# Half of the second batch's query and key projection moved into its first attention group, and two routings one group later

## The chip, the cores and the metric

The kernel runs on one core of a Trainium2 chip. A core has TensorE (PE, with its weight loads shown apart as PEld), VectorE (DVE), ScalarE (ACT), GpSimd (POOL) and SyncE (SP), each with a queue that it works through in order, and sixteen DMA engines. The metric is the device time of one launch in microseconds (us).

## The reference

The kernel computes one transformer layer on two batches of 2048 tokens with 256 channels. Cut to what matters:

```
qkv = (x @ Wqkv + bqkv).reshape(B, L, 3, 16, 16)
scores = einsum('bqhd,bkhd->bhqk', q, k) / 4 - slope[h] * |pos_q - pos_k|
x = layernorm(x + softmax(scores) @ v @ Wout + bout)
weights = softmax(x @ router_w.T + router_b)            # 8 experts, the last a no-op
per token the two best experts; each of 7 experts takes its first 512 tokens
x = layernorm(x + sum over its experts of weight * relu(x @ W1[e]) @ W2[e] + no-op part)
```

## The kernel before

**Attention.** The work is cut into units (b, g): batch b, group g of four heads; g counts from 0, so the change's "groups 3 and 4" are g = 2 and 3. A unit has four blocks n of 512 queries. (The last three units are split: blocks 0 to 2 of (1,1), (1,2), (1,3) come first, then their blocks 3.) A block is a row of steps. A step makes scores for two pairs of heads on PE (L699), their exponential on ACT (L707, mostly 128 x 1024), where the keys are near the queries a multiplication by a table of distances on DVE (L712), and two steps later the product with the values on PE (L615) into a PSUM accumulator. In groups 1 to 3 only a block's own four key tiles are multiplied by the table; group 0 (steep slopes) has few key tiles, and each piece of them is multiplied. At a block's end DVE divides (done), and after the odd group of a pair project_out adds the output projection to x_all (L509, L511). Score tiles and all side work share three PSUM tiles (tag st); accumulators have two.

**Projection.** project_qk(b, m, i, xb) makes queries and keys of a chunk i of 512 tokens for half m of the heads: m = 0 serves groups 0 and 1, m = 1 groups 2 and 3. For keys and then queries (a = 1, 0): two matmuls (L289), the high half hi with bias (L294 on ACT or L296 on DVE), the low half lo on DVE (L297), and their writes to DRAM (kd, qd) from SP (L300). Then POOL squares hi (L304), PE sums the squares (nrm, L310), and DVE takes the maximum (n, L317). project_v makes the values. project_all(b) (L349) goes over the four chunks and does m = 0, m = 1 and v of each; for batch 1 it is called second. find_flag (L361) reduces all these maxima, with two PE transposes in a chain with DVE, to a flag for a general path that is not taken here.

**Routing.** route(b, n) does for a block of 512 tokens: layer norm on DVE, transposes (rt, L745), logits (lg, L754), exponential (L784) and choice of the experts on DVE (some 25 small operations), counts (cnt, L826), slots on DVE, and eight scatters from POOL (L855). It starts when project_out of the second pair of groups has added its part.

**Order.** PE and ACT run in the order in which the program is written (manual_schedule, L880). DVE, POOL and SP are ordered by a scheduler at build time. Side work is written as generators: later(gen) puts one on a list, and pump (L488), called once at the end of each step, advances the first that is due; a generator that yields k is due k steps later, one that yields None lets the next one go. finish(gen) runs a generator to its end on the spot. second is put on the list after unit (0,1) and finished before the last block of (0,3), where the keys of (1,0) are loaded; find_flag is put on it after (0,3). After (1,0) the pools of the projection (x, hi, lo, sq) are closed, and the memory goes to the experts' weights (load_expert).

**Experts.** After attention seven experts run one after the other (L1195 to L1219), with gathers and scatters from POOL.

Of the kernel before, what the change touches and what calls it, by code (L numbers as in the profile page):

```python
# [22 lines left out]
G = 4  # L23
# [4 lines left out]
NQB = L // QB  # L28
# [94 lines left out]
def fast_path(  # L123
# [25 lines left out]
    def st_tile(name):  # L149
        return ps_st.tile([P, 2, QB], F32, tag="st", name=name)  # L150
# [23 lines left out]
    def load_x(b, i):  # L174
        xb = p_x.tile([P, 2, QB], F32, tag="xb", name=f"xb_{b}_{i}")
        nc.sync.dma_start(out=xb, in_=xt[b].rearrange("(c p) l -> p c l", p=P)[:, :, i * QB : (i + 1) * QB])
        return xb
# [103 lines left out]
    def project_qk(b, m, i, xb, queue=nc.sync):  # L281

        n0 = f"{b}_{m}_{i}"
        hi = p_s.tile([P, 2, QB], F32R, tag="hi", name=f"hi_{n0}")
        lo = p_s.tile([P, 2, QB], F32R, tag="lo", name=f"lo_{n0}")
        for a, dst in ((1, kd), (0, qd)):
            ps = st_tile(f"qk_{n0}_{a}")
            for c in range(2):
                nc.tensor.matmul(  # L289
                    ps[:, 0, :], wqk_sb[:, a, c, m * P : (m + 1) * P], xb[:, c, :], start=(c == 0), stop=(c == 1)  # L290
                )
            bias = bqk_sb[:, a, m : m + 1]
            if (b, m) == (0, 0):
                nc.scalar.activation(hi[:, a, :], ps[:, 0, :], AF.Identity, bias=bias)  # L294
            else:
                nc.vector.tensor_scalar(hi[:, a, :], ps[:, 0, :], bias, None, ALU.add)  # L296
            nc.vector.scalar_tensor_tensor(lo[:, a, :], ps[:, 0, :], bias, hi[:, a, :].bitcast(F32), ALU.add, ALU.subtract)  # L297
            for r, half in enumerate((hi, lo)):
                for to in (dst[b][m][i][:, c, :, r, :] for c in range(2)) if a else (dst[b][m][i][:, r, :, :],):
                    queue.dma_start(out=to, in_=half[:, a, :].bitcast(F32))  # L300
            yield 2
        sq = p_s1.tile([P, 2, QB], F32, tag="sq", name=f"sq_{n0}")
        hf = hi.bitcast(F32)
        nc.gpsimd.tensor_tensor(sq, hf, hf, ALU.mult)  # L304
        yield 6
        ps = st_tile(f"nrm_{n0}")

        for a in range(2):
            for c in range(4):
                nc.tensor.matmul(  # L310
                    ps[32 * c : 32 * c + 32, 0, a * P : (a + 1) * P],
                    blk,
                    sq[:, a, c * P : (c + 1) * P],
                    start=True,
                    stop=True,
                )
        nc.vector.tensor_reduce(  # L317
            n2[:, b, m, :, i], ps[:, 0, 0 : 2 * P].rearrange("p (a t) -> p a t", a=2), AX.X, ALU.max
        )
# [26 lines left out]
        if keep is not None:  # L346
            keep(vs)

    def project_all(b):  # L349
        xb = load_x(b, 0)  # L350
        for i in range(NQB):
            xb_next = load_x(b, i + 1) if i + 1 < NQB else None
            yield 1
            for m in range(2):
                yield from project_qk(b, m, i, xb)
                yield 2
            yield from project_v(b, i, xb)
            yield 2
            xb = xb_next

    def find_flag():  # L361

        mx = small.tile([P, 2, B, 2], F32, tag="mx", name="mx")
        top = small.tile([P, 1], F32, tag="mxt", name="mxt")
        for a in range(2):
            nc.vector.tensor_reduce(mx[:, a, :, :], n2[:, :, :, a, :], AX.X, ALU.max)
        nc.vector.tensor_reduce(top, vm.rearrange("p b i h -> p (b i h)"), AX.X, ALU.max)
        yield 4

        ps = st_tile("flag_s")  # L370
        for a in range(2):
            nc.tensor.transpose(ps[0:4, a, 0:P], mx[:, a, :, :].rearrange("p b m -> p (b m)"), ident)
        nc.tensor.transpose(ps[0:1, 0, P : 2 * P], top, ident)
        by_head = small.tile([4, 2, 32], F32, tag="mxh", name="mxh")
        nc.vector.tensor_reduce(by_head, ps[0:4, :, 0:P].rearrange("p a (c h) -> p a h c", c=4), AX.X, ALU.max)
        nc.vector.tensor_tensor(by_head[:, 0, :], by_head[:, 0, :], by_head[:, 1, :], ALU.mult)
        high = small.tile([4, 1], F32, tag="mx4", name="mx4")
        nc.vector.tensor_reduce(high, by_head[:, 0, :], AX.X, ALU.max)

        nc.vector.tensor_scalar(high, high, 0.99 / (4 * SMALL_SCORE) ** 2 / 0.98, None, ALU.mult)  # L380
        two = small.tile([1, 2], F32, tag="two", name="two")
        nc.vector.tensor_reduce(two[:, 0:1], ps[0:1, 0, P : 2 * P], AX.X, ALU.max)
        nc.vector.tensor_scalar(two[:, 0:1], two[:, 0:1], 1.0 / SMALL_V**2, None, ALU.mult)
        yield 4
        ps = st_tile("flag_t")
        nc.tensor.transpose(ps[0:1, 0, 0:4], high, ident[0:4, 0:4])
        nc.vector.tensor_reduce(two[:, 1:2], ps[0:1, 0, 0:4], AX.X, ALU.max)
        one = small.tile([1, 1], F32, tag="one", name="one")
        nc.vector.tensor_reduce(one, two, AX.X, ALU.max)
        nc.vector.tensor_scalar(bad[:, 0:1], one, 1.0, None, ALU.is_gt)  # L390
# [87 lines left out]
        return mixed(steps, own, 3 if n == 2 else 2)  # L478

    step = 0  # L480

    keys_in, queries_in, values_in = [0], [0], []
    waiting = []

    def later(gen, wait=0):
        waiting.append([step + wait, gen])
# [13 lines left out]
    def finish(gen):  # L500
        for w in [w for w in waiting if w[1] is gen]:
            waiting.remove(w)
        for _ in gen:
            pass
# [11 lines left out]
    def key_order(blocks):  # L516
        return (1, 2, 3, 0) if blocks[0] == 0 else (2, 1, 0, 3)
# [23 lines left out]
    def load_unit(b, g, blocks):  # L541
        ks, vu = unit_tiles(b, g, blocks)

        with tc.issue_after(last["q"].ins):
            for i in key_order(blocks):
                load_keys(b, g, i, ks)
            for i in range(NQB):
                load_values(b, g, i, vu)
        return ks, vu
# [173 lines left out]
    def route(b, n):  # L723
# [2 lines left out]

        rests = (5, 2, 2, 5) if (b, n) == (B - 1, NQB - 2) else (7, 3, 3, 9)
        while len(routed) < NQB * b + n - 1:
            yield None
        t0 = b * TB + 4 * n  # L730
        n0 = f"{b}_{n}"
# [195 lines left out]
    def first_blocks():  # L927


        one = project_qk(0, 0, 1, xbs[1])  # L930
        next(one)
        load_keys(0, 0, 1, ks)
# [61 lines left out]
        load_rest()  # L994
    make_fill()
    loaded = (ks, vu), first_tables, q_first
    second = project_all(1)
    for u, (b, g, blocks) in enumerate(units):
        (ks, vu), (e_t, f_t), q_t = loaded
        fs = None if f_t is None else (f_t[:, 0, :], f_t[:, 1, :])  # L1000
        va = va_first if u == 0 else None
        for n in blocks:
            if u in (1, 2):
                with tc.issue_after(last["q"].ins):
                    load_residual(NQB * (u - 1) + n)
            if u == 1 and n == 2:
                with tc.issue_after(last["q"].ins):
                    clear_slots()
            if g or va is None:
                va = values(b, g, n, vu)  # L1010
            if u == 0 and n + 1 in blocks:
                q_next = None
            elif n + 1 in blocks:
                q_next = load_q(b, g, n + 1)
            elif u + 1 < len(units):
                nb, ng, nblocks = units[u + 1]
                if (nb, ng) == (0, 2):
                    finish(other_half)
                if (nb, ng) == (1, 0):
                    finish(second)  # L1020
                nxt = load_unit(nb, ng, nblocks)
                q_next = load_q(nb, ng, nblocks[0])
            block(b, g, n, ks, va, e_t, fs, q_t)
            if q_next is None:
                while n + 1 not in queries_in:
                    pump()
                q_next = load_q(b, g, n + 1)
            q_t = q_next
        if u + 1 < len(units):
            loaded = nxt, load_tables(nb, ng), q_next  # L1030
        if (b, g) == (0, 1):
            later(second)
        if (b, g) == (0, G - 1):
            later(find_flag())
        if (b, g) == (1, 0):
            pctx.close()
            p_w = ctx.enter_context(tc.tile_pool(name="p_w", bufs=2, side="right"))
            expert_w = {0: load_expert(0)}
            p_x0 = ctx.enter_context(tc.tile_pool(name="p_x0", bufs=1, side="right"))
# [739 lines left out]
```

## Time and profile before

| what | us |
|---|---|
| median of three timed runs (1205.15 to 1208.55) | 1207.42 |
| the profiled execution, time | 1196.63 |
| its span, first to last instruction | 1194.8 |
| PE busy in it (93%) | 1114.9 |
| ACT busy (67%) | 796.7 |
| DVE busy (60%) | 714.6 |
| POOL busy (24%) | 284.5 |
| mean granted TensorE clock | 0.967 |

Units begin with their first exponential at 239.0 us (0,2), 382.6 (0,3), 541.4 (1,0), 620.5 (1,1), 695.8 (1,2) and 785.3 (1,3). A row of the profile's groups gives the line, engine, operation, output and inputs, shapes and count, then busy time and mean duration, then the idle time of the engine just before such instructions and what ended it. Shares of busy time over the whole span hide that the stages have different limits, so the stretches are looked at apart. A PE that is shown busy is not always at its peak, since the ends of matmuls are modelled.

### The profile page before, as it was taken

Reading aid. Unit: us, or ns where it says so; the run is one execution under the profiler, and the core shown is the slowest. Engines: PE = TensorE matmul, PEld = TensorE weight load, DVE = VectorE, ACT = ScalarE, POOL = GpSimd, SP = SyncE. Lnnn points to the kernel's source line nnn. Section 1 sums busy time; section 2 is a strip of 40 time slices with the busy share of each in tenths; the row PEclk is TensorE's granted clock in tenths of the full one; section 3 lists DMA queues with packets and bytes.
Section 4 is the critical chain, followed back from the end, with each engine's and each line's share of the span. In section 5 each row is a group of like instructions: output and inputs, shape, how many; then the busy total and the mean of one; then the engine's idle time right before and its main releaser. Section 6 shows DMA issues by size and latency. Waiting matters only on the chain. (4 is left out here: it accounts for less than half of the span.)

```text
span 1194.8 us, 19048 instructions
## 1 busy us (share of the span) xinstructions
PE 1114.9 (93%) x7174; PEld 495.6 (41%) x7174; DVE 714.6 (60%) x1525; ACT 796.7 (67%) x902; POOL 284.5 (24%) x304
## 2 busy tenths in 40 slices
PE   8788899999999999986989999999999999999996
PEld 3454334333323343433533333223334237666664
DVE  3738667754565467778985654446788543216534
ACT  4444588888887887673559999999886961112510
POOL 1111322222210112224164111111142402222253
PEclk9988899999999999997899999999999999999998
DMA  5648474342523314454334122122356413348721
GB/s 182 233 165 259 161 243 149 109 170 89 176 90 122 128 47 137 128 196 156 114 129 145 53 102 71 54 102 71 98 195 213 174 55 106 102 141 269 247 74 52
DMA packets 108147, 164.53 MB, mean 138 GB/s; under 512 B 28432, under 2 KB 59792, under 8 KB 108048
## 3 DMA queue, kind: packets, MB, share of 16 engines
q1 hardware_dynamic: 96960, 140.04, 36.0%
q0 software_dynamic: 5952, 16.49, 3.9%
q10 hardware_dynamic: 5136, 6.71, 1.7%
q8 instruction: 59, 0.97, 0.3%
q14 instruction: 40, 0.33, 0.1%
HBM read 108.86 MB, written 54.35 MB: 137 GB/s over the span
## 5 line engine op out<-in xcount | busy, mean ns | idle before, releaser
L707 ACT ACTIVATE pr<-s 128x1024 f32<-128x1024 f32 (+2 forms) x796 | 733.8, 1095 | 183.3 <-PE s L699 177.2
L712 DVE TENSOR_TENSOR pr<-pr,e 128x1024 f32<-128x1024 f32 (+16 forms) x366 | 341.8, 975 | 189.5 <-ACT pr L707 188.1
L699 PE MATMUL s<-q,k 64*128 64x512 f32 (+11 forms) x1852 | 330.2, 432 | 23.6 <-DMA k<-kd 8.3
L699 PEld LDWEIGHTS s<-q,k 64*128 64x128 f32 x1852 | 153.8, 189 | 334.3 <-ACT pr L707 229.9
L615 PE MATMUL acc_B<-pr,va 128*32 128x512 f32 (+5 forms) x1080 | 139.0, 570 | 0.0
L615 PE MATMUL acc_A<-pr,va 128*32 128x512 f32 (+8 forms) x1080 | 138.8, 569 | 0.0
L1202 ACT ACTIVATE ht<-h 128x1024 f32<-128x1024 f32 x28 | 28.7, 1023 | 143.5 <-PE h L1195 143.0
L615 PE MATMUL acc_D<-pr,va 128*32 128x512 f32 x768 | 113.5, 604 | 4.5 <-DVE wX L652 2.2
L589 POOL TENSOR_TENSOR va<-vu,fk_sb 128x768 f32<-128x768 f32 (+2 forms) x36 | 40.8, 1134 | 282.1 <-PE acc_D L615 267.3
L1216 PE MATMUL y<-w,ht 128*128 128x256 f32 x448 | 98.1, 379 | 2.2 <-DVE ye L1219 2.2
L1195 PE MATMUL h<-xet,w 128*128 128x512 f32 x224 | 97.9, 593 | 1.4 <-issue 1.4
L1216 PEld LDWEIGHTS y<-w,ht 128*128 128x128 f32 x448 | 84.6, 190 | 14.2 <-DVE ye L1219 2.6
L615 PE MATMUL acc_E<-pr,va 128*32 128x512 f32 (+15 forms) x696 | 69.5, 412 | 20.4 <-DVE pr L712 20.2
L855 POOL DMA_INDIRECT xbuf<-x_all,slot x56 | 62.2, 1110 | 97.4 <-DVE top L847 50.4
L304 POOL TENSOR_TENSOR sq<-hi 128x1024 f32<-128x1024 f32 x16 | 31.0, 1938 | 184.1 <-DVE hi L296 146.1
L289 PE MATMUL qk<-xb,wqk_sb 128*128 128x512 f32 x128 | 65.3, 633 | 1.1 <-ACT v L339 0.6
L1195 PEld LDWEIGHTS h<-xet,w 128*128 128x128 f32 x224 | 42.3, 190 | 50.8 <-issue 49.7
L1219 DVE SCALAR_TENSOR_TENSOR ye<-y,xe,sums 128x256 f32<-128x256 f32 x28 | 13.5, 484 | 64.7 <-PE y L1216 62.3
L1083 POOL DMA_INDIRECT sums<-abuf,to x28 | 26.9, 962 | 78.4 <-DVE to L1077 38.2
L615 PEld LDWEIGHTS acc_E<-pr,va 128*32 128x32 f32 x696 | 24.7, 117 | 46.6 <-DVE pr L712 22.0
L615 PEld LDWEIGHTS acc_B<-pr,va 128*32 128x32 f32 x1080 | 25.3, 108 | 42.5 <-issue 40.8
L615 PEld LDWEIGHTS acc_A<-pr,va 128*32 128x32 f32 x1080 | 24.8, 108 | 41.0 <-issue 39.2
(162 smaller groups left out, 870.5 us busy)
## 6 DMA issues: line engine op xcount, KB each, us to landing
k<-kd SPq DMA_DIRECT2D x86, 256.0 KB
e<-in_c_e SPq DMA_DIRECT2D x10, 1920.0 KB
q<-qd SPq DMA_DIRECT2D x62, 256.0 KB
w<-in_w SPq DMA_DIRECT2D x14, 1024.0 KB
kd<-hi SPq DMA_DIRECT2D x32, 256.0 KB
kd<-lo SPq DMA_DIRECT2D x32, 256.0 KB
xb<-in_xt SPq DMA_DIRECT2D x12, 512.0 KB
vu<-vd SPq DMA_DIRECT2D x40, 128.0 KB
```

Of the source, the lines that this page charges most:

```text
L289: nc.tensor.matmul(ps[:, 0, :], wqk_sb[:, a, c, m * P : (m + 1) * P], xb[:, c, :], start=(c == 0), stop=(c == 1))
L304: nc.gpsimd.tensor_tensor(sq, hf, hf, ALU.mult)
L589: nc.gpsimd.tensor_tensor(va[:, t0:t1, :, 0:HD], v4[:, t0:t1], fb, ALU.mult)
L615: nc.tensor.matmul(blk_["acc"](to)[32 * row : 32 * row + 32, q0:q1], blk_["va"][:, t, j, :], pr[:, jj, c0 : c0 + q1 - q0], start=key not i ...
L699: nc.tensor.matmul(ps[:, jj, c0 : c0 + q1 - q0], ks[hp][t // 4][r, t % 4 * P : (t % 4 + 1) * P], q_t[r, hp, q0:q1], start=True, stop=True,)
L707: nc.scalar.activation(pr[:, :, 0:w], ps[:, :, 0:w], AF.Exp, scale=1.0 / math.sqrt(HD))
L712: nc.vector.tensor_tensor(pc, pc, e_t[:, 2 * hp : 2 * hp + 2, x0 : x0 + q1 - q0], ALU.mult)
L855: nc.gpsimd.indirect_dma_start(out=xbuf_by[4 * k + u], out_offset=bass.IndirectOffsetOnAxis(ap=slot_i[:, k, u : u + 1], axis=0), in_=x_all ...
L1083: nc.gpsimd.indirect_dma_start(out=sums[:, s, :], out_offset=None, in_=abuf[:, :], in_offset=bass.IndirectOffsetOnAxis(ap=to[:, s : s + 1] ...
L1195: nc.tensor.matmul(ps[:, a, :], w1_sb[:, c, (2 * f + a) * P : (2 * f + a + 1) * P], xet[:, c, :], start=(c == 0), stop=(c == 1),)
L1202: nc.scalar.activation(ht[:, 2 * f : 2 * f + 2, :], ps, AF.Relu)
L1216: nc.tensor.matmul(ps, ht[:, f, s * P : (s + 1) * P], w2_sb[:, f, :], start=(f == 0), stop=(f == NC - 1))
```

## The change

- project_all is split. project_most(b) does for each chunk m = 0 and v. project_others(b) loads the chunks of x again and does m = 1, one step less apart, and then find_flag.
- second is now project_most(1), in its old place. third is project_others(1). It is put on the list after (0,3), where find_flag was, and finished before the last block of (1,0), where the keys of (1,1) are loaded.
- hi is made on ACT where b == m, so for (0, 0) as before and now for (1, 1); for (0, 1) and (1, 0) it is made on DVE as before.
- route(0, 2) and route(0, 3) wait until unit number 5, which is (1,1).

```diff
-            if (b, m) == (0, 0):
+            if b == m:
                 nc.scalar.activation(hi[:, a, :], ps[:, 0, :], AF.Identity, bias=bias)
...
-    def project_all(b):
+    def project_most(b):
+
         xb = load_x(b, 0)
         for i in range(NQB):
             xb_next = load_x(b, i + 1) if i + 1 < NQB else None
             yield 1
-            for m in range(2):
-                yield from project_qk(b, m, i, xb)
-                yield 2
+            yield from project_qk(b, 0, i, xb)
+            yield 2
             yield from project_v(b, i, xb)
             yield 2
             xb = xb_next
+
+    def project_others(b):
+        xb = load_x(b, 0)
+        for i in range(NQB):
+            xb_next = load_x(b, i + 1) if i + 1 < NQB else None
+            yield 1
+            yield from project_qk(b, 1, i, xb)
+            yield 1
+            xb = xb_next
+        yield from find_flag()
...
     step = 0
+    at_unit = 0
...
         while len(routed) < NQB * b + n - 1:
+            yield None
+
+        while (b, n) in ((0, 2), (0, 3)) and at_unit <= G:
             yield None
...
-    second = project_all(1)
+    second, third = project_most(1), project_others(1)
     for u, (b, g, blocks) in enumerate(units):
+        at_unit = u
...
                 if (nb, ng) == (1, 0):
                     finish(second)
+                if (nb, ng) == (1, 1):
+                    finish(third)
...
         if (b, g) == (0, G - 1):
-            later(find_flag())
+            later(third)
```

## The prediction

> **What bounds the kernel now.** I read the page's groups first, then busy time by stretch, then the timeline of the places the change touches. Counting the exponentials (L707, in program order) cuts the time into blocks (batch, group, block of queries). Rows of the stretches: start:end, length, then busy us of TensorE (PE), its weight loads, VectorE (DVE), ScalarE (ACT), GpSimd (POOL), then clock, DMA share, GB/s.
>
> ```profile
> L707 ACT ACTIVATE pr<-s 128x1024 f32<-128x1024 f32 (+2 forms) x796 | 733.8, 1095 | 183.3 <-PE s L699 177.2
> 239.02:278.19 39.17, 38.37 (x232) 12.82 (x224) 21.95 (x26) 30.10 (x33) 7.59 (x8) 1.00 0.42 143
> 278.19:311.06 32.87, 32.48 (x230) 11.57 (x232) 15.56 (x21) 29.55 (x32) 7.75 (x10) 1.00 0.30 100
> 311.06:347.60 36.54, 35.64 (x228) 10.88 (x224) 21.49 (x25) 30.05 (x34) 9.13 (x7) 1.00 0.44 135
> 347.60:382.61 35.01, 34.54 (x228) 12.11 (x228) 19.19 (x21) 29.86 (x33) 4.18 (x7) 1.00 0.35 113
> 382.61:417.71 35.10, 34.65 (x226) 10.65 (x224) 16.79 (x22) 29.83 (x33) 7.07 (x8) 1.00 0.43 149
> 417.71:455.89 38.18, 38.17 (x262) 15.93 (x260) 27.34 (x51) 30.21 (x33) 3.71 (x8) 1.00 0.14 45
> 455.89:499.90 44.01, 42.86 (x274) 16.82 (x272) 35.36 (x93) 30.40 (x33) 9.14 (x7) 0.96 0.44 137
> 499.90:541.35 41.45, 36.71 (x250) 15.59 (x252) 29.05 (x97) 29.96 (x33) 13.07 (x14) 0.96 0.54 184
> 541.35:620.52 79.17, 63.24 (x566) 31.48 (x566) 74.41 (x205) 37.44 (x46) 30.47 (x21) 0.83 0.39 129
> 642.13:669.07 26.94, 26.94 (x204) 10.09 (x200) 16.16 (x19) 25.29 (x29) 3.33 (x6) 1.00 0.29 78
> 695.84:726.28 30.44, 30.44 (x206) 10.05 (x208) 14.97 (x17) 29.19 (x34) 3.77 (x6) 1.00 0.28 99
> 726.28:755.39 29.11, 29.11 (x194) 8.87 (x192) 13.00 (x15) 29.11 (x34) 3.33 (x6) 1.00 0.25 73
> 814.26:848.29 34.03, 33.39 (x226) 12.57 (x224) 22.37 (x45) 30.35 (x34) 3.33 (x6) 1.00 0.23 63
> 848.29:881.85 33.56, 33.29 (x230) 12.76 (x228) 29.08 (x86) 29.88 (x35) 7.70 (x7) 1.00 0.39 120
> ```
>
> A block of 32 exponentials with nothing put in is 726.28:755.39: 29.1 us, ACT and PE both full. The first eight rows are the same blocks of (0,2) and (0,3), 33 to 44 us long: ACT is busy 30 us in each, and the rest is ACT waiting while PE works on what was put in between (177.2 of ACT's 183.3 us idle end on PE's scores). So **there every step put in costs span.** (1,0), the row 541.35, is different: DVE is busy 74.4 of 79.2 us, ACT under half. **There DVE is the bound.** (1,1) (642.13 is one block) is bound by PE and ACT again.
>
> Prices of what is put in, each block less 29.1: an output projection (o) 1.3 (695.84); nrm and two halves of v 3.8 (278.19); adding one half of qk to that 2.1 more (347.60); four halves of qk and nrm 7.4, three 6.0 (311.06, 382.61). I take 1.75 for a half of qk (1.4 to 2.1), 0.6 for nrm, 3.2 for v. o with rt and lg of a route is 4.9 (814.26), with cnt too 4.5 (848.29).
>
> **What leaves (0,2) and (0,3).** The built program's order gives the steps of each block. The first five blocks only swap steps: by the prices -0.3, +0.3, -0.9, +1.75, -2.05, in sum -1.2. (0,3,1) keeps o, rt, lg, like 814.26: 34.0 for 38.2, -4.2. (0,3,2) keeps o, cnt, rt, lg, like 848.29: 33.6 for 44.0, -10.4; the unspread end of the old projection goes with it. (0,3,3) keeps o and cnt, 29.1 + 1.3 + 0.8 = 31.2 for 41.5, -10.2; in it is a stall of 5.43 us (first row below: start, length, what ran, and in brackets the idle time before it and who ended it). It goes too, because the reduction of the value maxima (L367) now follows its producers in (0,3,0), ahead of POOL's scatters. The other rows are used further down:
>
> ```profile
> 510.83 0.17 DVE L367 TENSOR_REDUCE mxt<-vm 128x1 f32<-128x16 f32 x1 [5.43 <-POOL vm L343]
> 487.16 1.98 PE L289 MATMUL qk<-xb,wqk_sb 128*128 128x512 f32 x4
> 552.49 2.36 DVE L712 TENSOR_TENSOR pr<-pr,e 128x1024 f32<-128x1024 f32 x2 [0.69 <-DMA e<-in_c_e]
> 553.86 1.07 PE L615 MATMUL acc_E<-pr,va 128*32 128x512 f32 x2 [9.09 <-DVE pr L712]
> ```
>
> **Sum -26.0.** PE's own time gives a check: eight halves at 1.98, four nrm at 0.6, rt and lg at 1.1 and 1.95 are 21 us, and PE's wait for DVE there 4.2.
>
> **What (1,0) gets.** Per chunk of tokens: two halves of qk, two hi on ACT (688 ns; ACT is free), two lo on DVE (750), sq on POOL (1.9), nrm, a maximum (0.4), and on SP an xb load (512 KB, new: four more in all) and six writes at 0.6 to 1.0 us of issue. Nothing is queued behind the writes that is wanted soon but the keys and values of (1,1); the two experts' weights, moved behind them, are wanted after 950 us.
>
> Spread part: the pump advances once a step, a chunk asks for twelve steps, and (1,0) has twenty before the finish ahead of its last block. So only chunk 0 and most of chunk 1 are spread. From (1,0) DVE loses some 44 small route operations lying between the multiplications (0.09 each, 4.0), the xr copy with its gap (2.2), the flag's chain (1.5), and what POOL's kept and va cost it (two multiplications took 2.68 and 3.31 for 1.4 and 1.5: 3.0): -10.7. It gains three lo (2.1; the fourth lies under the wait of the last fence), a maximum (0.4), two sq on POOL beside multiplications (a multiplication beside a POOL operation took 1.89 for 1.22: 1.4), and PE brings four qk for the rt, lg and cnt gone, 1.5: +5.4. Net -5.3. The softmax of route 2 that leaves the start brings nothing: there everything waits for the table e (issued 542.97, used 552.49), which still starts when the last multiplication of (0,3) ends.
>
> Unspread part: in the built program, between (1,0,2) and (1,0,3), PE's queue holds nrm 1, qk 2, nrm 2, qk 3, nrm 3 and the flag's transposes, in that order, before any score of (1,0,3). PE runs in order, so **a chain through four engines stands in front of all attention work**: nrm 1 0.6; twice (4.0 qk + 0.15 + 0.7 hi + 0.1 + 1.9 sq + 0.1 + 0.6 nrm) = 15.1; maxima, transposes, flag on DVE, its last transpose 3.4 (this chain took 1.3 on DVE alone at 564.6); scores, first exponential 1.6: 20.7. DVE still holds some 2.3 of multiplications when it begins: DVE's stop is 18.4.
>
> Then the clock. The Trainium skill, TensorE: Matmul & The Clock Gate, section Why this matters for your kernels, warns of idle gaps over about 3 us between bursts of matmuls, after which PE runs at half rate. The gaps of this chain are 2.9 us each, so by the letter nothing is added. The row of (1,0) speaks against the letter: mean clock 0.83, with 0.51 at 581 to 586 us and 0.58 at 597 to 600, where PE's gaps just before are 2.0 us and less. Half clock throughout doubles 8 us of qk. Between 0 and 8 I take 4. **(1,0): -5.3 + 18.4 + 4 = +17** (range 9 to 24).
>
> **What (1,1) gets.** rt, lg, cnt of two routes, less the one cnt there before: 2.2 + 3.9 + 0.8 = 6.9 of PE, or 3.6 + 3.1 by the rows 814.26 and 848.29 against 695.84. PE and ACT are full (642.13), so it all counts: 7. Further, both softmaxes, some 50 DVE operations at 0.14, stand in DVE's queue of (1,1,1) after the output transpose and before the x_all addition and wB. PE needs wB's accumulator for acc_X about 8 us into the block; DVE comes to it at about 5 + 7 + 1.9 = 14. Meanwhile the PSUM tile of o is held as well. +6, bounds 0 (the queue had slack) and 8. The 16 scatters move to POOL in (1,1,1) and (1,1,2), 10 us a route, ahead of parts of va for (1,2,0), whose need is 15 us later: nothing; uncovered, up to 5. **(1,1): +13** (7 to 17).
>
> **Sum: -26 + 17 + 13 = +4.** The profiled execution took 1196.6 us (span 1194.8), so it would be about 1200.6. The median of the runs is 1207.4; the differences are carried over to it: **1211**.
>
> **Rivals.**
> - *The run is cheap, faster*: place, the run between (1,0,2) and (1,0,3). If the pump got further, or PE and POOL overlapped more than the order shows, and the clock held, the stop falls from 22 to about 12; with (1,1) at 9 the sum is -26 + 7 + 9 = -10: 1197. It decides as soon as stop plus acc_X wait fall by more than 8. For it: the sure gain is the largest term, read from whole blocks. Against: PE's written order.
> - *No change*: the stop without half clock, acc_X waiting 4: -26 + 13 + 11 = -2: 1205.
> - *The run is dearer*: sq 2 stands on POOL behind va of (1,1,0), which waits for values that SP issues behind k loads and behind writes waiting for lo; I find it landed some 4 us before sq 2 is due. If it is late by 10, 1221.
> - *It does not do what it says*: the program's order shows route 2 and 3 moved and eight hi on ACT; only the spreading is partial.
>
> **Numbers.** Forecast 0.45, cheap run 0.27, no change 0.13, dear run 0.15. From no change this kernel's measurement tells about 0.3%, 3.6 us. Of the forecast's own spread (1205 to 1217) a quarter lies within that band or under. Slower 0.56, same 0.16, faster 0.28. The gain's bounds (-21 to -30) and those of (1,0) and (1,1) give 1196 to 1223.
>
> **What would show it.** The eight blocks of (0,2) and (0,3) about 276 us for 302; (1,0) about 96 for 79, with 18 to 24 us in which ACT has only four hi; PE on acc_X waiting for wB in (1,1,1); the DVE wait at L367 gone. A stop under 12 us, or (1,1) unchanged, would make the prediction wrong.

## The result, and the profile after

The changed kernel takes **1223.0 us** (median of 4 runs, 1222.0 to 1229.0) beside 1206.3 of the kernel before (1201.5 to 1208.6): **ratio 1.0156** over the runs, 95% interval 1.012 to 1.0191 (the two medians alone give 1.0138). It is slower. Its profiled execution took 1222.55 us, its span 1220.7, the mean granted clock 0.957 (before: 1196.63, 1194.8, 0.967).

The group of the exponentials on the page of the changed kernel (busy us, mean ns, idle us before them):

```profile
L718 ACT ACTIVATE pr<-s 128x1024 f32<-128x1024 f32 (+2 forms) x796 | 734.6, 1090 | 186.7 <-PE s L710 167.0
```

Its busy time by stretch (start:end, length, then busy us of PE, PEld, DVE, ACT, POOL, then clock, DMA share, GB/s). The stretches are the eight blocks of (0,2) and (0,3), then (1,0) as a whole, then (1,1,0), (1,1,1) and (1,1,2), cut at first exponentials as before.

```profile
236.35:275.89 39.54, 38.37 (x240) 14.32 (x232) 22.20 (x26) 30.21 (x33) 7.78 (x9) 1.00 0.40 141
275.89:308.44 32.55, 32.17 (x218) 10.04 (x216) 16.70 (x21) 29.65 (x33) 7.74 (x9) 1.00 0.29 97
308.44:344.58 36.14, 35.72 (x222) 12.32 (x224) 19.95 (x24) 29.78 (x33) 7.76 (x8) 1.00 0.50 150
344.57:381.18 36.61, 36.26 (x232) 12.65 (x224) 21.00 (x25) 30.05 (x34) 5.60 (x7) 1.00 0.35 117
381.18:414.04 32.86, 32.47 (x230) 11.84 (x232) 14.86 (x19) 29.49 (x33) 3.71 (x8) 1.00 0.35 121
414.04:447.72 33.68, 33.04 (x224) 12.40 (x216) 22.02 (x45) 30.00 (x34) 3.33 (x6) 1.00 0.05 15
447.72:481.29 33.57, 33.29 (x230) 12.77 (x228) 28.99 (x86) 29.87 (x35) 7.73 (x7) 1.00 0.32 97
481.29:513.61 32.32, 30.86 (x210) 10.16 (x212) 25.90 (x84) 29.88 (x33) 10.81 (x10) 1.00 0.25 82
513.61:606.54 92.93, 72.89 (x634) 36.31 (x626) 72.96 (x152) 42.45 (x51) 18.05 (x16) 0.87 0.61 202
606.54:631.40 24.86, 23.26 (x196) 11.32 (x194) 12.82 (x14) 19.63 (x22) 3.33 (x6) 1.00 0.44 159
631.40:672.01 40.61, 36.48 (x224) 15.20 (x224) 25.41 (x80) 26.29 (x31) 7.11 (x8) 0.79 0.24 75
672.01:710.60 38.59, 30.21 (x202) 10.94 (x202) 21.97 (x48) 25.97 (x28) 18.79 (x20) 0.91 0.29 94
```

ACT's idle time is as long as before, 186.7 us for 183.3: what the exponentials no longer wait for in (0,2) and (0,3) they wait for elsewhere. The eight blocks sum to 277.3 us for 302.3: **-25.1**. (1,0) takes 92.9 for 79.2: **+13.8**. (1,1) takes 104.1 for 75.3: **+28.7**, of which +3.3, +13.7 and +11.8 in its three blocks. Before, (1,1,0) and (1,1,2) were these rows:

```profile
620.52:642.13 21.61, 19.08 (x174) 8.50 (x176) 13.29 (x30) 19.70 (x23) 13.27 (x15) 1.00 0.51 183
669.07:695.84 26.77, 26.02 (x200) 9.70 (x192) 18.39 (x21) 25.30 (x29) 3.33 (x4) 1.00 0.18 61
```

In the last two blocks PE's clock is now 0.79 and 0.91 where it was full, and in the very last neither PE (30.2 of 38.6) nor ACT (26.0) nor DVE (22.0) is full. The blocks of (1,2) and (1,3) that follow, up to their fourth, are the same to 0.1 us.

The timeline of three places of it, as rows of start, length, what ran, and in brackets the idle time before it:

```profile
404.70 0.16 DVE L377 TENSOR_REDUCE mxt<-vm 128x1 f32<-128x16 f32 x1
...
525.00 7.04 DVE L723 TENSOR_TENSOR pr<-pr,e 128x1024 f32<-128x1024 f32 x9 [4.19 <-DMA e<-in_c_e]
...
573.42 3.70 PE L289 MATMUL qk<-xb,wqk_sb 128*128 128x512 f32 x8
580.12 0.64 PE L310 MATMUL nrm<-sq,first_sb 128*32 128x128 f32 x16 [3.00 <-POOL sq L304]
580.69 5.40 PE L289 MATMUL qk<-xb,wqk_sb 128*128 128x512 f32 x8
588.90 0.64 PE L310 MATMUL nrm<-sq,first_sb 128*32 128x128 f32 x16 [2.81 <-POOL sq L304]
```

The reduction that had waited 5.43 us behind POOL's scatters waits for nothing. The run of chunks stands in (1,0) as four rows of PE with gaps of 3 us, and the table e is still what (1,0) begins with.

In (1,1,1) PE's longest wait is for the output addition, which DVE reaches behind the softmaxes of the two routes. Rows of PE and DVE, then two stretches of the block:

```profile
632.48 0.79 PE L710 MATMUL s<-q,k 64*128 64x512 f32 x2 [1.18 <-ACT pr L718]
652.13 1.22 DVE L522 TENSOR_TENSOR x_all<-o,x_all 128x1024 f32<-128x1024 f32 x1
653.36 0.68 DVE L668 TENSOR_TENSOR wB<-acc_B,f 128x512 f32<-128x512 f32 x1
653.40 1.22 PE L710 MATMUL s<-q,k 64*128 64x512 f32 x4 [2.95 <-DVE x_all L522]
...
631.99:642.23 10.24, 9.75 (x44) 5.28 (x44) 3.95 (x11) 3.40 (x4) 0.45 (x1) 0.50 0.55 155
652.47:659.30 6.83, 5.90 (x24) 1.40 (x24) 1.73 (x5) 3.88 (x4) 1.90 (x1) 0.50 0.38 131
```

The clock is one half in both, 17 of the 40.6 us; the first of these stretches begins before any softmax of the block.

The two profiles differ by 25.9 us, more than the medians (16.7). Of this 9.3 us lie after 896 us, in the fourth blocks of (1,1), (1,2) and (1,3), which the change does not touch. The first comparison shows why.

### The profile page after: what moved, and what is told of

Read it like the earlier page. It is cut to its first block, busy times and chain, and to the rows that moved or that the text cites. A ratio compares the mean times of both kernels' runs of the same rounds, so it can differ in the third digit from the quotient of the medians.

```text
span 1220.7 us, 19063 instructions
## 1 busy us (share of the span) xinstructions
PE 1126.0 (92%) x7174; PEld 501.4 (41%) x7174; DVE 708.6 (58%) x1517; ACT 802.6 (66%) x910; POOL 274.7 (23%) x304
## 3 DMA queue, kind: packets, MB, share of 16 engines
q1 hardware_dynamic: 98048, 142.13, 35.8%
## 4 chain that ended last, share of the span: by engine, by line
PE 68%; DVE 14%; ACT 7%; issue 5%; DMA 4%; SPq 1%; POOL 0%; another core or an unknown queue 0%; ACTq 0%; POOLq 0%; DVEq 0%
PE s L710 18%; PE acc_A L626 8%; DVE pr L723 8%; PE h L1212 7%; PE acc_B L626 7%; PE y L1233 7%; PE acc_D L626 7%; ACT pr L718 7%; PE qk L289 3%; PE v L328 3%; PE o L520 2%; PE acc_E L626 2%; PE lg L768 1%; DMA kd<-lo 1%; DMA y<-abuf 1%
## 5 line engine op out<-in xcount | busy, mean ns | idle before, releaser
L718 ACT ACTIVATE pr<-s 128x1024 f32<-128x1024 f32 (+2 forms) x796 | 734.6, 1090 | 186.7 <-PE s L710 167.0
L723 DVE TENSOR_TENSOR pr<-pr,e 128x1024 f32<-128x1024 f32 (+16 forms) x366 | 337.9, 971 | 189.2 <-ACT pr L718 177.8
L710 PE MATMUL s<-q,k 64*128 64x512 f32 (+11 forms) x1852 | 338.5, 440 | 41.9 <-DMA k<-kd 9.1
L710 PEld LDWEIGHTS s<-q,k 64*128 64x128 f32 x1852 | 157.0, 192 | 365.3 <-ACT pr L718 249.5
L626 PE MATMUL acc_B<-pr,va 128*32 128x512 f32 (+5 forms) x1080 | 143.4, 585 | 0.0
L1219 ACT ACTIVATE ht<-h 128x1024 f32<-128x1024 f32 x28 | 28.7, 1024 | 145.0 <-PE h L1212 127.0
L626 PE MATMUL acc_D<-pr,va 128*32 128x512 f32 x768 | 117.0, 620 | 4.5 <-DVE wX L663 3.0
L869 POOL DMA_INDIRECT xbuf<-x_all,slot x56 | 57.1, 1020 | 88.3 <-DVE top L861 73.2
L626 PE MATMUL acc_E<-pr,va 128*32 128x512 f32 (+16 forms) x696 | 62.5, 395 | 13.4 <-DVE pr L723 13.4
L626 PEld LDWEIGHTS acc_B<-pr,va 128*32 128x32 f32 x1080 | 25.9, 110 | 43.3 <-issue 41.8
L1109 POOL DMA_INDIRECT abuf<-ye,to x24 | 23.3, 970 | 75.7 <-DVE ye L1236 58.1
```

The costliest lines, as they stand in the source:

```text
L626: nc.tensor.matmul(blk_["acc"](to)[32 * row : 32 * row + 32, q0:q1], blk_["va"][:, t, j, :], pr[:, jj, c0 : c0 + q1 - q0], start=key not i ...
L710: nc.tensor.matmul(ps[:, jj, c0 : c0 + q1 - q0], ks[hp][t // 4][r, t % 4 * P : (t % 4 + 1) * P], q_t[r, hp, q0:q1], start=True, stop=True,)
L718: nc.scalar.activation(pr[:, :, 0:w], ps[:, :, 0:w], AF.Exp, scale=1.0 / math.sqrt(HD))
L723: nc.vector.tensor_tensor(pc, pc, e_t[:, 2 * hp : 2 * hp + 2, x0 : x0 + q1 - q0], ALU.mult)
L869: nc.gpsimd.indirect_dma_start(out=xbuf_by[4 * k + u], out_offset=bass.IndirectOffsetOnAxis(ap=slot_i[:, k, u : u + 1], axis=0), in_=x_all ...
L1219: nc.scalar.activation(ht[:, 2 * f : 2 * f + 2, :], ps, AF.Relu)
```

## E1: the change in halves, and both kernels again

All four on one chip, where the kernel before took 1209.1 us. First the two kernels themselves:

> The kernel before, unchanged, for a second profile. Theory: its profiled execution of 1196.6 us lay under its own median, and the code after 880 us, which the change does not touch, varies: the three stretches with the fourth blocks of queries of (1,1), (1,2), (1,3) take 96 to 102 us instead of 92.3, and the whole about 1206. Rival: they take 92 to 93 again, so that the 9.3 us that these stretches lost in the changed kernel belong to the change.

> The changed kernel, unchanged, for a second profile. Theory: (0,2)+(0,3) 277 us, (1,0) 93, (1,1) 104 again within 3 us each, the stretches of the fourth blocks under 97. Rival: the stops of 3 us in (1,1,2) in which all engines stand were an accident of one execution, and (1,1) takes 95 or less.

The kernel before came to 1210.0, ratio 1.0003 (0.9986 to 1.002); the changed one to 1223.4, ratio **1.0117** (1.0083 to 1.0151). Rows of the second profile of before: (1,0), (1,1,0), then all of the fourth blocks:

```profile
535.81:615.59 79.78, 61.67 (x566) 31.52 (x565) 74.06 (x205) 37.75 (x46) 32.69 (x21) 0.84 0.39 128
615.59:643.54 27.95, 21.70 (x174) 9.49 (x176) 13.63 (x30) 20.15 (x23) 11.91 (x15) 0.86 0.39 140
...
883.12:983.75 100.63, 88.11 (x606) 31.53 (x604) 62.35 (x163) 80.11 (x88) 31.37 (x32) 0.97 0.49 167
```

The fourth blocks take 100.6 us here, against 92.3 in the first profile of before and 101.5 and 102.2 in the two of the changed kernel (under 97 was expected of it), and 92.2 in its order on the chip of E2 (e2_scatter_spread): the 9.3 us are not the change's. Block (1,1,0) takes 27.95 for 21.61. What differs can be counted in the trace. For each of the 796 exponentials, take the time from the moment when ACT was free and its scores' last matmul had ended to its start. In the first profile of before none of them is over 0.4 us; in the second 8 are over 1 us, up to 3.4 us; in the two of the changed kernel 5 and 9, up to 5.0 and 6.0. All of these lie beside POOL's trains of eight or sixteen scatters (each about 1 us, one every 1.27 us) or start within 2 us of a train's end. So **what waits for TensorE while GpSimd scatters can start late**, and the first profile of before happened not to show it. That the scatters are the cause is not shown yet; E4 tests it.

Pair against pair on this chip: (0,2)+(0,3) 302.0 to 277.3, (1,0) 79.8 to 93.0, (1,1) 81.5 to 106.8, fourth blocks 100.6 to 102.2. These sum to +15.4, nearly all of the 16.1 us between the two spans (1204.9 and 1221.0).

**The routes alone.** The kernel before with only the hold:

```diff
+        while (b, n) in ((0, 2), (0, 3)) and at_unit <= G:
+            yield None
```

> The kernel before with only the routes of blocks (0,2) and (0,3) held back to (1,1). Theory (what the changed kernel's trace shows): (1,1) goes from 75 to about 103 us by the routes alone, (0,3) loses 4 and (1,0) 8 to 10: the sum is +14 to +18, about 1221. Rival (the price of the prediction): (1,1) +13, so that the sum is -1 to +2, about 1207.

Ratio **1.0073** (1.0044 to 1.0102). (0,2)+(0,3) lose 1.7 us, (1,0) 12.8, and (1,1) goes from 81.5 to 103.1. The theory is right that (1,1) pays this length for the routes, whatever else moves. About the sum neither side is right: by the ratio it is 8.8 us, between the 14 to 18 of the theory and the -1 to +2 of the rival.

**The projection alone.** The changed kernel without those two lines:

> The changed kernel without the routes' hold: only the projection of the second half of q and k moves, and ScalarE takes the high halves. Theory: (1,1) stays at 75 to 79 us; (0,2)+(0,3) about 279; (1,0), which keeps the routes and gets the run of chunks, about 103 (79 + 14 + 10): sum about +1, 1208. Rival: the length of (1,1) comes from the projection (late keys, the clock after the run): (1,1) stays over 90, and the whole is 1220 or more.

Ratio **1.0102** (1.0075 to 1.0128). (1,1) takes 76.2 us, so the length of (1,1) does not come from the projection, as the theory said. But (1,0) takes 120.0, not 103, so the theory missed the whole by its size for (1,0). At 1224.3 us the whole is where the rival had it (1220 or more), but not by the rival's cause. Its timeline, rows of POOL and one of PE, shows what happens in the run:

```profile
589.68 0.97 POOL L866 DMA_INDIRECT xbuf<-x_all,slot  x1 [0.30 <-issue]
590.67 1.51 POOL L600 TENSOR_TENSOR va<-vu,fk_sb 128x768 f32<-128x768 f32 x1
592.11 0.40 POOL L603 COPY va<-vu 128x256 f32<-128x256 f32 x1
592.47 1.89 POOL L304 TENSOR_TENSOR sq<-hi 128x1024 f32<-128x1024 f32 x1
...
594.41 1.08 PE L310 MATMUL nrm<-sq,first_sb 128*32 128x128 f32 x16 [8.52 <-POOL sq L304]
```

The squares that nrm needs stand in POOL's queue behind eight scatters and va, and PE stands 8.5 us. The halves are not additive: alone they cost 0.7% and 1.0%, together 1.2%, since the hold takes the routes, scatters and all, from in front of the run (27.0 us in (1,0)) and sets them down in (1,1) (30.6 us more there than without it).

## E2: no scatters, scatters singly, the run spread

On a second chip, where the kernel before took 1194.5 us.

```diff
-        for u in range(4):
+        for u in range(4 if (b, n) not in ((0, 2), (0, 3)) else 0):
             for k in range(2):
                 nc.gpsimd.indirect_dma_start(
```

> The changed kernel without the 16 scatters by GpSimd of the routes of (0,2) and (0,3) (what they write, those tokens' rows in the experts' buffer, is left out). Theory: the trains of scatters hold the block (1,1,2) up, where exponentials start 2 to 6 us after the scores they read: (1,1,2) falls from 40 us to 27 to 30, (1,1) from 104-107 to 92-95, and the whole to about 1211 from 1223. Rival: DVE's slot operations and the wait for the x_all addition do it: (1,1,2) stays at 37 or more, the whole at 1220 or more.

Block (1,1,2) takes 28.3 us, (1,1) 93.8. What follows the last exponential of attention, the experts, is 8 to 9 us longer with those rows missing (230.0 us, for 220.6 to 222.5 in the profiles of the changed kernel), so the whole, ratio 1.0131 (1.0079 to 1.0183), says nothing. And the block says less than it seems: on this chip **no** exponential starts over 0.4 us late in any of the four profiles, and a kernel with all its scatters has 28.1 in the same block (below). The test cannot decide here; E4 has it on another chip.

```diff
                     in_offset=None,
                 )
+                if (b, n) in ((0, 2), (0, 3)):
+                    yield 2
```

> The changed kernel with the scatters of the routes of (0,2) and (0,3) given out one at a time, two steps apart. Theory (the price belongs to the train of eight back to back): single scatters cost little, the stretch (1,1,1) to (1,2,2), 170 us in the changed kernel (41 + 40 + 89), falls to 158 to 162, the whole to about 1213. Rival (each scatter has its price, some 0.8 us, wherever it stands): the stretch stays at 168 or more, the whole at 1221 or more.

Ratio **1.006** (1.0041 to 1.008). It was no test of what it was meant for: in its trace the scatters still start 1.27 us apart. POOL's queue holds little else there, and it takes the next as soon as the slots are known; a place further down in the program is not a later time. But up to (1,1,2) it is the changed kernel, and shows it on a chip without the delay: (0,2)+(0,3) 277.3, (1,0) 92.8, (1,1) 93.3.

**The run spread.** project_qk gets its two rests as an argument, and project_others asks for the least, so that all four chunks fit into the steps of (1,0):

```diff
-            yield from project_qk(b, 1, i, xb)
-            yield 1
+            yield from project_qk(b, 1, i, xb, rests=(0, 1))
```

> The changed kernel with shorter rests in the second projection, so that its four chunks all lie between the steps of the first three blocks of (1,0) and none is left for the run ahead of the last block. Theory: the run's stop of 18 to 20 us goes and comes back only as far as DVE has work, (1,0) falls from 93 to 72-78, the whole to about 1205. Rival: DVE and TensorE pay for the chunks in the spread as well: (1,0) stays at 87 or more, the whole at 1217 or more.

Ratio **0.9945** (0.9926 to 0.9965), 1188.6 us. Rows of (1,0), (1,1,1), (1,1,2):

```profile
515.96:597.90 81.94, 68.11 (x634) 33.29 (x626) 72.87 (x140) 42.34 (x52) 18.63 (x16) 0.94 0.71 238
...
622.76:661.86 39.10, 35.57 (x224) 14.98 (x224) 25.48 (x80) 26.44 (x31) 7.11 (x8) 0.83 0.24 71
661.86:689.99 28.13, 26.87 (x202) 10.06 (x202) 21.77 (x48) 25.68 (x28) 19.80 (x20) 1.00 0.37 123
```

(1,0) does the same work as in the changed kernel (DVE 72.9 us in both) in 11 us less: that is what the run costs against spreading it. It stays 2.8 us above the kernel before and above the 72 to 78 expected: the spread chunks are not quite free. POOL's 19.8 us in the last row are the scatters, and the block takes 28.1.

> The same shorter rests without holding the routes back. Theory: (1,0), 120 us with the run, falls to 95-100; (1,1) takes 77 to 82, since some of the third route's work slides into it; (0,2)+(0,3) stay at 280: the whole about 1204, below the kernel before. Rival: routes and projection together fill DVE in (1,0): it takes 110 or more, the whole 1215 or more.

Ratio 1.0019 (1.0001 to 1.0037): (1,0) 100.1, (1,1) 78.7, (0,2)+(0,3) 280.1, each at or within 0.1 us of what the theory said, but the whole is no gain over the kernel before on this chip. With the run spread, holding the routes back is worth more than not.

## E3: one softmax later

On a third chip, where the kernel before took 1206.2 us.

> The changed kernel again, beside the next three on one chip. Theory: the delay behind trains of scatters belongs to some chips. Where exponentials start late behind trains, (1,1,2) takes 39 to 41 us and the ratio to the kernel before is 1.011 to 1.016; where they do not, (1,1,2) takes 28 and the ratio is 1.004 to 1.008. Rival: the delay belongs to the order of this kernel, and (1,1,2) takes 39 to 41 on every chip.

Ratio 1.0118 (1.0074 to 1.0162), (1,1,2) 40.6 us, with 4 late exponentials, two of them in it: as the theory says of a chip that delays.

> The changed kernel with the scatters of (0,2) and (0,3) given out singly, two steps apart, now beside the changed kernel on one chip. Theory: where the trains delay, (1,1,2) falls from 40 to 28-31 and the whole by 8 to 12 us; where they do not, it gains and loses at most 2 us. Rival: the same number of scatters costs the same however it is given out: no difference on either chip.

Ratio 1.0133 (1.0087 to 1.018). The stretch from (1,1,1) to (1,2,2) is 167.4 us for 170.8; the second train has moved into (1,2,0), which takes 36.0 for 30.5. Since the scatters are not apart in time, neither side is tested.

```diff
         rests = (5, 2, 2, 5) if (b, n) == (B - 1, NQB - 2) else (7, 3, 3, 9)
+        if (b, n) == (0, 3):
+            rests = (7, 3, 13, 9)
```

> The projection spread over (1,0) as before, and the softmax of the route of (0,3) put ten steps later, behind the output addition, wB and wX of (1,1,1). Theory (two softmaxes ahead of the addition and of wB hold TensorE up and cost it its clock): (1,1,1) falls from 39-41 us to 33-35, (1,1,2) rises by 1 to 2. Rival (the work of rt, lg and cnt itself, and the clock lost before): (1,1,1) stays at 38 or more.

Ratio **0.9927** (0.989 to 0.9965). (1,1,1) takes 35.5 us, just above the range, (1,1,2) 30.95, (1,0) 81.9.

The larger gain is one that neither side expected: (1,1,2), which was to rise by 1 to 2 us, falls from 40.6. The second softmax takes its route's scatters with it. In the changed kernel sixteen follow one another (676.5 to 698.2 us in e3_after); here they are two trains of eight, 663.5 to 673.9 and 687.2 to 697.8, and no exponential of (1,1,2) is late, on a chip that delays. Whether the parting of the trains does it is not tested: the projection is spread here too.

> All three: projection spread over (1,0), the second softmax later, the scatters given out singly. Theory: (1,0) 82, (1,1) about 87, no late exponentials behind trains in (1,1): 12 us under the kernel before where trains delay that one, 9 to 12 under it where they do not; ratio 0.990 to 0.993. Rival: the single scatters and the later softmax push the later routes, and what (1,1) saves is given back in (1,2) and (1,3): ratio 0.995 or more.

Ratio 0.9947 (0.9927 to 0.9967): (1,0) 81.9, (1,1) 91.6 instead of 87, and (1,2,0) 36.65. The second train stands in (1,2,0), as in e3_scatter_spread, and takes back what was saved, with an exponential 2.6 us late beside the train; the rival is nearer.

## E4: the scatters again, where they delay

On a fourth chip, where the kernel before took 1206.3 us.

> The changed kernel beside the next three on one chip: (1,1,2) 39 to 41 us where exponentials start late behind trains of scatters, 28 where they do not; (1,1,1) 40 to 41 on either.

> The changed kernel without the 16 scatters of the routes of (0,2) and (0,3) (their rows of the experts' buffer are left out). Theory: on a chip where (1,1,2) of the changed kernel takes 39 to 41 us, it takes 27 to 30 without the scatters, and (1,1) falls by 10 to 13. Rival: DVE's slot operations and the PSUM tile held by the x_all addition do it, and (1,1,2) stays at 37 or more. On a chip without the delay both give 28, which tells nothing.

This chip delays: 8 exponentials of the changed kernel start over 1 us late, three of them in (1,1,2), and 4 of the other, all beside the trains that it still has. Ratios 1.0092 (1.0057 to 1.0128) and 1.0113 (1.0078 to 1.0148), the second with 7.7 us more in the expert stage. Block (1,1,2) as busy time of the stretch, in the changed kernel:

```profile
675.13:710.68 35.55, 29.65 (x202) 10.72 (x202) 21.88 (x48) 25.93 (x29) 19.60 (x20) 0.95 0.30 105
```

and without the scatters:

```profile
674.51:702.85 28.34, 26.93 (x202) 10.06 (x202) 21.99 (x48) 25.68 (x28) 2.94 (x4) 1.00 0.16 55
```

Its exponentials on ACT's timeline, in the changed kernel:

```profile
675.13 9.92 ACT L718 ACTIVATE pr<-s 128x1024 f32<-128x1024 f32 x10
690.67 3.58 ACT L718 ACTIVATE pr<-s 128x896 f32<-128x896 f32 x4 [5.63 <-PE s L710]
694.43 1.94 ACT L718 ACTIVATE pr<-s 128x1024 f32<-128x1024 f32 x2 [0.17 <-PE s L710]
698.10 3.92 ACT L718 ACTIVATE pr<-s 128x1024 f32<-128x1024 f32 x4 [1.73 <-PE s L710]
703.85 7.88 ACT L718 ACTIVATE pr<-s 128x1024 f32<-128x1024 f32 x9 [1.82 <-PE s L710]
```

and without the scatters:

```profile
674.51 10.01 ACT L718 ACTIVATE pr<-s 128x1024 f32<-128x1024 f32 x10
686.76 17.14 ACT L718 ACTIVATE pr<-s 128x896 f32<-128x896 f32 x19 [2.25 <-PE s L710]
```

POOL goes from 19.6 to 2.9 us, DVE keeps its slot operations (48 instructions in both), and the block loses 7.2 us: ACT waits once and then runs through. **The scatters are the cause, not DVE's slot operations.** The size is less than expected (39 to 41 us with them, 10 to 13 us for (1,1); (1,1) goes from 101.0 to 93.95). The block without them is what it is on the chip that does not delay. What it is of a scatter, GpSimd's own work or the transfers (DMA share 0.30 with them, 0.16 without), is not separated. Block (1,1,1), ahead of the scatters, is 40.6 and 40.75.

> The spread projection with the softmax of the route of (0,3) ten steps later, repeated for its interval. Theory: (1,1,1) 35 to 36 us again, (1,1,2) 28 to 31, ratio to the kernel before 0.990 to 0.995. Rival: the first ratio, 0.9927, was luck, and it lies at 0.997 or more.

Ratio 0.9961 (0.9938 to 0.9984), with 35.8 and 30.96 us in the two blocks. The two blocks repeat; the ratio lies above the 0.990 to 0.995 that was said, and under the rival's 0.997.

> As e4_stagger, with the softmax of (0,2) six steps later too, behind the addition and wB of (1,1,1), and that of (0,3) after it. Theory: no softmax is left ahead of them, TensorE waits for neither, (1,1,1) falls from 35 to 30-32, (1,1,2) takes 29 to 31, ratio 0.985 to 0.990. Rival: the softmaxes then stand ahead of the same operations of (1,1,2) and take there what (1,1,1) saves: (1,1,1)+(1,1,2) stays at 64 to 67.

Ratio 0.9937 (0.9915 to 0.996). Rows of (1,1,1), (1,1,2), (1,2,0):

```profile
613.07:642.55 29.48, 29.24 (x226) 12.51 (x224) 18.77 (x45) 25.40 (x30) 3.33 (x6) 1.00 0.21 56
642.55:679.91 37.36, 31.13 (x204) 10.89 (x204) 29.22 (x66) 26.08 (x31) 15.98 (x14) 0.91 0.29 101
679.91:715.98 36.07, 33.37 (x210) 10.73 (x212) 17.96 (x36) 29.89 (x33) 11.58 (x14) 0.91 0.32 118
```

With no softmax ahead of the addition and of wB, (1,1,1) takes 29.5 us at full clock: its own 27 and the work. So far the theory: of the 13.7 us that (1,1,1) had gained, 11.1 go. Not all of them are the order of DVE's queue. The two counts, 0.7 us each on PE, have moved on to the next blocks; spreading the projection had taken 1.4 (40.5 to 39.1, E2); and the half clock at the start of the block, ahead of the softmaxes, is still there with one softmax moved (a mean clock of 0.83 in (1,1,1) of e3_stagger) and goes only with this edit, which also moves the transposes rt of (0,3) three steps. What the one softmax is worth is 3.6 us, a count included (39.1 to 35.5); the rest is shared and not separated.

And the rival has the sum: the two blocks take 66.8 us, and (1,2,0) another 5.6 more; the ratio is above the 0.985 to 0.990 of the theory. That the softmaxes alone do it is not shown: each of (1,1,2) and (1,2,0) also has a train of scatters, and beside it an exponential that is 4.4 and 2.3 us late. Between e4_stagger2, e4_stagger and e2_spread_gate the intervals overlap. All three are below the kernel before, on each chip on which they ran.

## Why the prediction was wrong

It forecast slower, by 4 us; it is slower by 12 to 17. The direction was right, the size was not.

- **(0,2) and (0,3): right.** -26.0 was said, -25.1 and -24.7 measured. By the prices of single steps: (0,3,1) -4.2 said, -4.5 measured; (0,3,2) -10.4 and -10.4; (0,3,3) -10.2 and -9.1; the first five blocks -1.2 and -1.0. The wait of 5.43 us went as said, and nothing came in its place.
- **(1,0): right in mechanism, 3 to 4 us too dear.** +17 was said, +13.8 and +13.2 measured. On PE the chain stood in the order and with the gaps given (3.0 and 2.8 us for 2.9), and DVE did no multiplication from 574.9 to 594.0, 19.1 us for 18.4. The 4 us for a lost clock were too much: of the two qk pairs in the run one took 3.70, one 5.40 us, so 1.7. What is left for the spread part is a saving of some 7 us (an estimate: 13.8 less 19.1 and 1.7), more than the 5.3 said. With all four chunks spread (1,0) takes 81.9, 2.8 above before, so the chunks taken out of the run cost some 10 us there (the same estimate): they are not free. The 2.68 and 3.31 us given for two multiplications beside POOL stand in no row; the rows have 2.32 us for 576 columns (0.74 elsewhere) and 1.92 for 32 (0.2), some 3.3 us too long together, so the 3.0 taken for them holds.
- **(1,1): this step failed.** +13 was said (7 to 17); measured +28.7, and +25.3 pair against pair on one chip; that (1,0) was too dear hid 3 to 4 us of it. The term that failed was: "The 16 scatters move to POOL in (1,1,1) and (1,1,2), 10 us a route, ahead of parts of va for (1,2,0), whose need is 15 us later: nothing; uncovered, up to 5." As to va it was right; nobody waited for it. The runs show another cost: on three of four chips exponentials and the output addition beside the trains start 1 to 6 us after the TensorE work that they need. In (1,1,2), where PE and ACT hand over to each other at every step and nothing else is full, that took 7.2 us in E4, the one removal on a chip that delays; in E1 and E3 the block is 12 to 13 above 28.3. In the kernel before these trains stood in the DVE-bound (1,0) and in (1,1,0), which is 6.3 longer with late exponentials on the chip of E1 than without in the first profile.
- **The rest of (1,1): the term was mis-sized.** Without scatters (1,1) takes 93.8 to 94.0, 18.5 to 18.6 above the first profile of before, for 13. The wait behind two softmaxes was put at 6, from DVE reaching wB 14 us into (1,1,1). It reached the addition 20.7 and wB 22.0 us in (652.13 and 653.36), since it waited itself for lg and the last accumulator, and the clock of 0.79, which was priced in (1,0) only, came on top. What PE waits for is not acc_X behind wB, as was said, but the PSUM tile that the addition frees (2.95 us), which the prediction had named in passing.
- **The sum on the profile of before.** It was made against an execution without late exponentials, while the medians come from chips that have them. That hid what a scatter can cost from every row the prices were taken from. On the second chip, which has none, the kernel with the same order up to (1,1,2) has the ratio 1.006, 7 us: nearer to the forecast. In part that is luck: the 3 us too much in (1,0) stand there against 5 too little in (1,1).
- **The rivals.** The dear run gave 1221, close to the time measured, but by another cause: its wait of sq on POOL is not in the changed kernel. It is in the one without the hold (8.5 us behind eight scatters and va). The cheap run needed the chunks to be spread further, which the written order excluded; with the rests shortened, it gives 0.9945.

What stays open is how a scatter makes its neighbours late. The end of a TensorE instruction in the trace is modelled, so the profile does not tell whether PE ended late or its signal came late; nor does anything here tell one chip from another, or a chip from the hour at which its runs were made, since each set stands on one chip at one time.

## What to carry to other kernels

Work moved off a full stage is paid for again where it lands: look for the queue it stands in there (the squares behind the scatters, the addition behind the softmaxes) before adding up busy times, and spread it in steps rather than leave it to a finish on the spot, which on the chip of E2 was the difference between 0.6% lost and 0.5% won. Two trains of GpSimd scatters in a block where TensorE and ScalarE answer each other at every step cost 7.2 us in E4; whether they would cost less in a stage with one other engine as its bound, no run tests. Take a second profile of the kernel before, from the chip on which the comparison runs, before pricing rows of the first.

## What the hardware showed unexpectedly

- In the changed order no exponential of 796 starts over 0.4 us late on one chip, and 4 to 9 start over 1 us late on the others; the kernel before takes 1194.5 us on that chip and 1206 to 1209 on the others.
- A block with 16 scatters takes 28.1 us on the one (POOL 19.8 us busy) and 35.6 to 41.2 on the others, with the same instructions: their starts are late.
- A full clock in (1,1,1) (29.5 us) against 0.79 (40.6) for nearly the same matmuls. In the slow one PE stands still for over 0.2 us only twice, 1.18 us up to 632.48 and 2.95 up to 653.40, 4.1 us in all, while its busy time is 7.2 us longer (36.5 for 29.2, the two counts' 1.4 included): the clock, one half for 10.2 and 6.8 us beside these gaps, costs more than the gaps. The Trainium skill, TensorE: Matmul & The Clock Gate, section Why this matters for your kernels, warns of gaps over about 3 us; here one of 1.18 and one of 2.95 us stand at the beginning of a stretch at half clock.
